# A graph layer on one core: the copy of the transposes goes from ScalarE to VectorE, 56 columns a step in place of 52, columns from step 12 in place of 18

## The chip, the cores and the metric

The kernel runs on one core of one Trainium2 chip. The metric is the device time of one execution in microseconds; lower is better. Engines are named as the profile names them: PE (TensorE), DVE (VectorE), ACT (ScalarE), POOL (GpSimd), SP (SyncE, which only issues transfers here). A row with a "q" behind the engine (ACTq, DVEq, SPq) belongs to that engine's sequencer: what it issues or loads into its registers.

## The reference, cut to what matters

```python
x, src, dst, ef          # 12500 x 64 nodes; 212500 edges, sorted by dst; 212500 x 32 edge features
msg  = relu(concat(x[src], x[dst], ef) @ mW1 + mb1) @ mW2 + mb2     # hidden width 128
agg  = segment_sum(msg, dst, 12500)
upd  = relu(concat(x, agg) @ uW1 + ub1) @ uW2 + ub2
out  = layernorm(x + upd)                                           # over the 64 features
```

Everything is float32. The kernel sums the hidden rows after the relu and multiplies by `mW2` (folded into `uW1`) only once per node.

## The kernel before, in words

The edges are cut into 554 groups of 384 (three tiles of 128 edges). Since the edges are sorted by destination, the edges of one group end in a window of at most 32 nodes. The first matmul of a group has 128 contraction rows: 64 features of the source node, 32 rows of a one-hot of the destination within the window, 32 edge features. Its weights `own_wm` hold the matching rows of `mW1` and, in the middle, 32 rows of the table `by_dst` (the product of every node with the destination part of `mW1`), loaded anew for each group (`window`, L430).

**Steps.** The main loop makes one step per group. Step k does on PE three parts of three groups: `turn(k)` transposes the gathered rows and the one-hots of group k (L466, three transposes into the PSUM tile `own_ps`); `hidden(k-3)` multiplies the operand columns of group k-3 by `own_wm` (L492, into `own_pre`); `sums(k-6)` adds the relu'd rows of group k-6 by the one-hots (L521, into `own_ps` behind the transposes). Behind the step ACT copies the transposes and the sums in one instruction from `own_ps` into `own_operands` (L479, 96 rows or, for a group whose features come as columns, 32 rows, by 513 elements). DVE makes the relu (L503, 128 x 384, `own_pre` to `own_h`) and the one-hots of group k+6 (L440, `own_rows`). SP stores the sums in one of two node tables `by_node` (L455) and loads the window of group k+4.

**Where the features come from.** There are three ways. POOL gathers rows of `x` from HBM with one indirect transfer per tile (L194), `AHEAD` groups ahead of the step, into a ring of `RING` groups. SP fetches two single rows a step for the third tile of 8 groups (L783, `own_side`). And for 71 of the 554 groups ("columned" groups) nothing is gathered: the whole transposed node table lies in SBUF (`own_xc`, each column behind a column of zeros, so that two nodes can be joined by an addition), and DVE and ACT copy the 384 columns one source node at a time. Each step copies 52 columns of the next columned group: DVE 28 as 14 additions of two columns each (L725, parts of 12, 8 and 8), ACT 24 one at a time (L728, parts of 8, 4, 4, 4, 4). The addresses of the columns are known only at run time: ahead of each part its engine loads that many addresses into registers with one TENSOR_LOAD (L702, eight steps' addresses lie in one `index` tile).

**What sets the order.** The order on each engine is written out by hand, in the order of the calls in the loop. `step` waits on PE for the last users of the PSUM slots and for the operands; `follow` issues what comes behind a part. The start differs: until step 15 each step also loads one sixteenth of the node table (`bit`: `src_sb` L256 and `own_xc` L258 on SP, a row of ones L235 on ACT), since a column may come from any node, columns begin only at step `BEGIN` = 18, when all bits are in. Until step 24 each step makes 512 rows of `by_dst` (`projected`: PE L407, ACT copy L410 into one of three buffers `t`, store L411 on SP). `window` waits for every store of `by_dst` issued so far. At step 8 (`CHECKED`) DVE checks once that the edges are sorted. Every 22 or 23 groups 512 nodes are complete, and `update` runs for them in twelve stages, one per step: both tables read back (`found`), joined on PE (L571), a count and a relu on ACT (L588, L621), a copy on DVE (L598), and the norm (L637 to L652). In the last ten steps (`SHORT`) the parts of a step run apart, without columns.

## Time and profile before

| | |
|---|---|
| three timed runs | 1846.92 to 1851.61 us, median 1848.74 us |
| the profiled execution's own time | 1847.94 us |
| its span | 1846.2 us |
| granted PE clock, mean over the span | 0.939 |
| busy share of PE, DVE, ACT, POOL | 76%, 62%, 87%, 74% |
| moved by DMA | 137.63 MB |

How to read it: "busy" counts instructions that the engine executes. Register loads and the issuing of transfers belong to the sequencers and are not counted as busy, so an engine can be held up with a low busy share. Rows of a timeline give start and length in us, then in brackets the idle time ahead of the row and what ended it; neighbouring rows of one kind are merged ("x24"). Rows of one line give its durations as minimum, median and maximum in ns, and then the starts of its first and its last instruction.

### The profile page before, as it was taken

How to read it: one execution, taken by the hardware profiler on the slowest of the kernel's cores; microseconds unless marked ns; L12 is line 12 of the kernel's file. 1: busy time of each engine (PE TensorE's matmuls, PEld its weight loads, DVE VectorE, ACT ScalarE, POOL GpSimd, SP SyncE). 2: the span in 40 equal slices, each digit the busy share in tenths (PEclk: the TensorE clock that was granted, in tenths of full speed). 3: DMA queues.
4: the chain of work that ended last, by engine and by line, in shares of the span. 5: the costliest groups of instructions: out<-in, count | busy, mean ns of one | idle time of the engine just before them, and what ended most of it. 6: DMA issues, size and time to landing. Idle time of an engine off the chain costs nothing. (4 is left out here: it accounts for less than half of the span.)

```text
span 1846.2 us, 57017 instructions
## 1 busy us (share of the span) xinstructions
PE 1402.9 (76%) x9841; PEld 1112.0 (60%) x9841; DVE 1151.3 (62%) x9034; ACT 1602.8 (87%) x13268; POOL 1362.1 (74%) x1447
## 2 busy tenths in 40 slices
PE   3677677877878878768778778777778778788677
PEld 3565565666656656556566566656656556566565
DVE  2315566666666666666666666666666666666652
ACT  2338799999999999899999999989999989989962
POOL 7777577777777777777777777777777777777772
PEclk9759899999999999999999999999989999999999
DMA  6653333333333333333333333333323333333331
GB/s 148 137 132 90 69 74 65 69 76 65 69 75 66 73 72 64 72 61 74 74 65 70 75 64 69 74 64 68 78 63 67 76 63 69 76 63 70 75 65 39
DMA packets 197393, 137.63 MB, mean 75 GB/s; under 512 B 62855, under 2 KB 172653, under 8 KB 196957
## 3 DMA queue, kind: packets, MB, share of 16 engines
q1 hardware_dynamic: 150166, 85.91, 18.7%
q0 software_dynamic: 46080, 47.25, 15.5%
q14 instruction: 288, 2.35, 0.4%
q8 instruction: 85, 1.39, 0.3%
q10 hardware_dynamic: 774, 0.72, 0.2%
HBM read 105.70 MB, written 28.00 MB: 72 GB/s over the span
## 5 line engine op out<-in xcount | busy, mean ns | idle before, releaser
L194 POOL DMA_INDIRECT own_rows<-in_x,src_sb x1440 | 1361.3, 945 | 451.0 <-issue 191.1
L728 ACT ACTIVATE own_operands<-own_xc 64x1 f32 x12576 | 1288.7, 189 | 16.5 <-issue 5.0
L725 DVE TENSOR_TENSOR own_operands<-own_xc 64x2 f32 x7344 | 666.9, 149 | 499.7 <-issue 496.3
L466 PE MATMUL own_ps<-own_ident,own_rows 128*96 128x128 f32 x1653 | 297.8, 292 | 329.9 <-ACT own_operands L728 208.6
L521 PE MATMUL own_ps<-own_h,own_rows 128*32 128x129 f32 x3322 | 491.3, 285 | 4.1 <-ACT own_operands L479 1.9
L492 PE MATMUL own_pre<-own_wm,own_operands 128*128 128x128 f32 x3322 | 490.2, 287 | 0.0
L466 PEld LDWEIGHTS own_ps<-own_ident,own_rows 128*96 128x96 f32 x1653 | 173.0, 133 | 460.4 <-ACT own_operands L728 273.1
L492 PEld LDWEIGHTS own_pre<-own_wm,own_operands 128*128 128x128 f32 x3322 | 443.8, 203 | 2.3 <-issue 1.4
L479 ACT ACTIVATE own_operands<-own_ps 96x513 f32<-96x513 f32 (+2 forms) x554 | 321.1, 580 | 96.0 <-PE own_ps L521 68.5
L503 DVE TENSOR_SCALAR own_h<-own_pre 128x384 f32<-128x384 f32 x553 | 300.4, 543 | 148.2 <-PE own_ps L521 106.9
L521 PEld LDWEIGHTS own_ps<-own_h,own_rows 128*32 128x32 f32 x3322 | 330.5, 113 | 82.7 <-issue 8.6
L440 DVE TENSOR_TENSOR own_rows<-iota,dlc 128x96 f32<-128x96 f32 x554 | 133.7, 242 | 0.1
L571 PE MATMUL u_ps<-own_ident,found 128*1 128x128 f32 (+1 forms) x768 | 100.2, 281 | 19.4 <-DMA found<-by_node 19.0
L571 PEld LDWEIGHTS u_ps<-own_ident,found 128*1 128x1 f32 (+1 forms) x768 | 74.4, 138 | 36.6 <-issue 14.7
L407 PE MATMUL u_ps<-w1b,own_xc 65*128 65x128 f32 x196 | 41.6, 375 | 51.1 <-DMA own_xc<-in_xT_spaced 22.6
L410 ACT ACTIVATE t<-u_ps 128x512 f32<-128x512 f32 (+1 forms) x25 | 14.7, 587 | 70.9 <-DMA by_dst<-t 38.9
L407 PEld LDWEIGHTS u_ps<-w1b,own_xc 65*128 65x128 f32 x196 | 35.4, 268 | 58.3 <-issue 30.5
L576 PE MATMUL u_ps<-own_xc,ux 65*128 65x512 f32 (+1 forms) x50 | 28.5, 650 | 24.1 <-DVE agg L598 24.1
L627 PE MATMUL u_ps<-same,own_xc 65*128 65x64 f32 x192 | 39.6, 288 | 0.5 <-ACT u L621 0.5
L616 PE MATMUL u_ps<-agg,wc 128*128 128x512 f32 (+1 forms) x50 | 39.8, 890 | 0.0
L628 PE MATMUL u_ps<-u,u 128*128 128x64 f32 x192 | 37.1, 275 | 0.0
L627 PEld LDWEIGHTS u_ps<-same,own_xc 65*128 65x128 f32 x192 | 30.3, 197 | 5.7 <-issue 4.2
(92 smaller groups left out, 312.8 us busy)
## 6 DMA issues: line engine op xcount, KB each, us to landing
own_operands<-in_efT SPq DMA_DIRECT2D x138, 192.0 KB
own_rows<-in_x,src_sb POOLq DMA_INDIRECT x1440
by_node<-own_operands SPq DMA_DIRECT2D x554, 32.2 KB
own_side<-in_x SPq DMA_DIRECT2D x1024, 0.2 KB
found<-by_node SPq DMA_DIRECT2D x46, 258.0 KB
own_wm<-by_dst SPq DMA_DIRECT2D x554, 16.0 KB
by_dst<-t SPq DMA_DIRECT2D x24, 256.0 KB
own_xc<-in_xT_spaced SPq DMA_DIRECT2D x12, 358.5 KB
```

Source lines behind the costliest of these rows:

```text
L194: nc.gpsimd.indirect_dma_start(out=s[:p, j, :D], out_offset=None, in_=x[:, :], in_offset=bass.IndirectOffsetOnAxis(ap=src_sb[:p, g * TG + ...
L407: nc.tensor.matmul(ps[:, j], xc[: D + 1, base + j * P :][:, :P], w1b, start=True, stop=True)
L440: places_by[g] = nc.vector.tensor_tensor(own.s[g % RING][:, :, D:], iota.unsqueeze(1).to_broadcast([P, TG, W]), dlc[:, g * TG : (g + 1) * ...
L466: nc.tensor.transpose(xt[:, j * P : j * P + p], sides[g] if g in sides and j == TG - 1 else s[:p, j, :], ident[:p, :p])
L479: after(nc.scalar.activation(t[r, c : c + n], ps[r, AT : AT + n], AF.Copy), step))]
L492: nc.tensor.matmul(pre[:p, j, :], t[:, c + j * P : c + j * P + p], wm[g % NW], start=True, stop=True)
L503: relu_by[g] = [nc.vector.tensor_scalar(h, pre, 0.0, None, ALU.max)]
L521: nc.tensor.matmul(ps[D : D + W, BANK : BANK + ROW], s[:p, j, D:], h[:p, j, :], start=j == 0, stop=j == len(sizes) - 1)
L571: nc.tensor.matmul(ps[:, k * P : (k + 1) * P], t[:, k, w], ident, start=j == 0, stop=j == 1)
L627: nc.tensor.matmul(y[:p, k], xc[: D + 1, nodes[k]], same, start=True, stop=False)
L725: by[engine] = nc.vector.tensor_tensor(o, one, other, ALU.add)
L728: by[engine] = nc.scalar.activation(o, x_at, AF.Copy)
```

## The change

- `tensor_copy` on DVE takes the place of ACT's copy of the transposes (L479 before, L482 and L483 after) for the groups 16 to 543; the first 16 and the last 10 stay on ACT.
- ACT copies 28 columns a step (8, 4, 4, 4, 4, 4), one part of four more; with DVE's 28 that is 56 a step.
- Columns begin at step 12. 77 groups get their features as columns, so POOL has 18 gathers less.
- The sixteen bits of the node table are loaded two per step in the steps 0 to 7; the load of the far part of `dst_cols` goes from ahead of the loop to step 1, and the arithmetic on it (`relative`) to step 8.
- `window(g)` waits only for the stores of `by_dst` of the chunks up to `max(1, g - 6)`, and `t` has four buffers.
- In a step with all three parts the relu of `hidden` is recorded (`later`) behind the first six additions of columns, not behind the step.
- The gathers run 15 groups ahead, not 16 (ring of 19), the small tiles of the check lie in a spare row of `own_xc`, and the first nodes as floats are kept in `first_i`. The nodes 11776 to 12287 are updated as 128 and 384, not 256 and 256.

```diff
-AHEAD = 16
+AHEAD = 15
 RING = AHEAD + 4
...
-BEGIN = 18
+BEGIN = 12
 CHECKED = 8
 VCOLS = (12, 8, 8)
-ACOLS = (8, 4, 4, 4, 4)
+ACOLS = (8, 4, 4, 4, 4, 4)
...
-    for e in [*range(CH, whole, CH), whole - CH // 2, whole, N]:
+    for e in [*range(CH, whole, CH), whole - CH * 3 // 4, whole, N]:
...
-    rowp = ctx.enter_context(tc.tile_pool(name="rows", bufs=3))
+    rowp = ctx.enter_context(tc.tile_pool(name="rows", bufs=4))
...
-        written.append(after(nc.sync.dma_start(
-            by_dst[base : base + n * P, :].rearrange("(n p) h -> p n h", n=n), t[:, :n])))
+        written[c] = after(nc.sync.dma_start(
+            by_dst[base : base + n * P, :].rearrange("(n p) h -> p n h", n=n), t[:, :n]))
...
-        after(wm_by[g], *written, *([hidden_by[g - NW]] if g >= NW else []))
-        written.clear()
+        needed = [written.pop(c) for c in sorted(written) if c <= max(1, g - 6)]
+        after(wm_by[g], *needed, *([hidden_by[g - NW]] if g >= NW else []))
...
-            copies = [ordered_by_steps(
-                after(nc.scalar.activation(t[r, c : c + n], ps[r, AT : AT + n], AF.Copy), step))]
+            out_t, in_ps = t[r, c : c + n], ps[r, AT : AT + n]
+            copies = [ordered_by_steps(after(
+                nc.vector.tensor_copy(out_t, in_ps) if NEAR_GROUPS <= g < G - SHORT
+                else nc.scalar.activation(out_t, in_ps, AF.Copy), step))]
...
-            users[part][(g + ahead_of[part]) % SLOTS] = follow(did[-1])
+            def followed(part=part, g=g, follow=follow):
+                users[part][(g + ahead_of[part]) % SLOTS] = follow(did[-1])
+
+            if part is hidden and len(parts) == 3:
+                later.append(followed)
+            else:
+                followed()
...
-    nc.sync.dma_start(dlc_i[:, near:], a["dst_cols"][:, near:])
     update_weights()
     weights(NW)
     inputs(1)
-    relative(NEAR_GROUPS, G)
...
-        if k < BITS:
-            bit(k)
+        for i in range(2 * k, min(2 * k + 2, BITS)):
+            bit(i)
         if 1 < k < len(TABLE):
             projected(k)
+        if k == 1:
+            nc.sync.dma_start(dlc_i[:, near:], a["dst_cols"][:, near:])
         if k == CHECKED:
+            relative(NEAR_GROUPS, G)
...
         fetch(0)
+        while later:
+            later.pop()()
         window(k + SB)
```

On DVE one step in the middle of the program stands like this before (`own_h` is the relu, `own_operands<-own_xc` the additions of columns, `own_rows` the one-hots):

```order
L503 TENSOR_SCALAR own_h<-own_pre 128x3x128
L702 TENSOR_LOAD index
L725 TENSOR_TENSOR own_operands<-own_xc 64x2 x6
L440 TENSOR_TENSOR own_rows<-iota,dlc 128x3x32
L702 TENSOR_LOAD index
L725 TENSOR_TENSOR own_operands<-own_xc 64x2 x4
L702 TENSOR_LOAD index
L725 TENSOR_TENSOR own_operands<-own_xc 64x2 x4
```

And a step at the same place of the changed program:

```order
L482 COPY own_operands<-own_ps 96x513
L706 TENSOR_LOAD index
L729 TENSOR_TENSOR own_operands<-own_xc 64x2 x6
L507 TENSOR_SCALAR own_h<-own_pre 128x3x128
L442 TENSOR_TENSOR own_rows<-iota,dlc 128x3x32
L706 TENSOR_LOAD index
L729 TENSOR_TENSOR own_operands<-own_xc 64x2 x4
L706 TENSOR_LOAD index
L729 TENSOR_TENSOR own_operands<-own_xc 64x2 x4
```

The copy stands where the relu stood, ahead of the load of 12 addresses, and the relu stands behind the six additions that this load serves.

On ACT a step before is the copy (L479) and five parts of columns, each behind its load of 8 or 4 addresses:

```order
L479 ACTIVATE own_operands<-own_ps 96x513
L702 TENSOR_LOAD index
L728 ACTIVATE own_operands<-own_xc 64x1 x8
L702 TENSOR_LOAD index
L728 ACTIVATE own_operands<-own_xc 64x1 x4
L702 TENSOR_LOAD index
L728 ACTIVATE own_operands<-own_xc 64x1 x4
L702 TENSOR_LOAD index
L728 ACTIVATE own_operands<-own_xc 64x1 x4
L702 TENSOR_LOAD index
L728 ACTIVATE own_operands<-own_xc 64x1 x4
```

In the changed program it is six parts of columns and no copy:

```order
L706 TENSOR_LOAD index
L732 ACTIVATE own_operands<-own_xc 64x1 x8
L706 TENSOR_LOAD index
L732 ACTIVATE own_operands<-own_xc 64x1 x4
L706 TENSOR_LOAD index
L732 ACTIVATE own_operands<-own_xc 64x1 x4
L706 TENSOR_LOAD index
L732 ACTIVATE own_operands<-own_xc 64x1 x4
L706 TENSOR_LOAD index
L732 ACTIVATE own_operands<-own_xc 64x1 x4
L706 TENSOR_LOAD index
L732 ACTIVATE own_operands<-own_xc 64x1 x4
```

One load of four addresses and four columns came, one copy with a wait on PE went.

On SP one early step before (load of a bit, store of `by_dst`, window, store of sums):

```order
L256 DMA src_sb<-in_src 128x101
L258 DMA own_xc<-in_xT_spaced 64x1436
L411 DMA by_dst<-t 128x4x128
L430 DMA own_wm<-by_dst 32x512
L455 DMA by_node_181<-own_operands 64x516
```

And step 7 of the changed program:

```order
L257 DMA src_sb<-in_src 128x101
L259 DMA own_xc<-in_xT_spaced 64x1434
L257 DMA src_sb<-in_src 128x101
L259 DMA own_xc<-in_xT_spaced 64x1436
L413 DMA by_dst<-t 128x4x128
L432 DMA own_wm<-by_dst 32x512
L457 DMA by_node_176<-own_operands 64x516
```

Two bits stand ahead of the store where one stood. On POOL the gathers before and after are these:

```order
L194 DMA own_rows<-in_x,src_sb 128x64 x1439
L194 DMA own_rows<-in_x,src_sb 20x64
```

```order
L195 DMA own_rows<-in_x,src_sb 128x64 x1421
L195 DMA own_rows<-in_x,src_sb 20x64
```

1440 became 1422.

More of the change, by code (lines that the diff above doesn't have):

```diff
@@ L150, in ordered @@
     ident, wm = own.ident, own.wm
+    spare = own.xc[96:97, :]
     xc = own.xc[:, 1 : 2 * NP + 1].rearrange("p (n s) -> p n s", s=2)[:, :, 0]
@@ L276, in ordered @@
     halves = [(0, G // 2), (G // 2, G)]
-    firsts_f = [own.pre[k][:, : g1 - g0] for k, (g0, g1) in enumerate(halves)]
+    all_firsts = first_i.bitcast(F32)
+    firsts_f = [all_firsts[:, g0:g1] for g0, g1 in halves]
     for f, (g0, g1) in zip(firsts_f, halves):
@@ L293, in ordered @@
     relative(0, NEAR_GROUPS)
-    high = temp.tile([1, G], F32, name="high")
+    high = spare[:, 0 * G : 1 * G]
     nc.vector.memset(high, float(N - 1))
@@ L298, in ordered @@
         nc.vector.memset(high[:, g0:g1], float(CH * (1 + max(1, g0 - 6)) - W))
-    start_f = temp.tile([1, G], F32, name="start_f")
+    start_f = spare[:, 1 * G : 2 * G]
     start_b = const.tile([1, G, 2], I32, name="start_b")
@@ L338, in ordered @@
     store_by = {}
-    written = []
+    written = {}
     up = found_p = None
@@ L356, in ordered_edges @@
         nc.vector.tensor_scalar(off, dlc, W - 1.0, 0.0, ALU.is_le, ALU.add, accum_out=valid[:, 1:2])
-        low = temp.tile([1, G], F32, name="low")
+        low = spare[:, 2 * G : 3 * G]
         opens = [0, *(closes for *_, closes in PLAN)]
@@ L363, in ordered_edges @@
         nc.vector.memset(high[:, 0:1], 0.0)
-        wrong = temp.tile([1, 2, G], F32, name="wrong")
+        wrong = spare[:, 3 * G : 5 * G].rearrange("o (k g) -> o k g", k=2)
         nwrong = temp.tile([1, 2], F32, name="nwrong")
         first_f = start_f
-        nc.vector.tensor_copy(first_f, first_i[0:1, :])
+        nc.vector.tensor_copy(first_f, all_firsts[0:1, :])
         nc.vector.tensor_tensor(wrong[:, 0], first_f, low, ALU.is_lt)
@@ L803, in ordered @@
     ahead_of = {turn: 0, hidden: TO_HIDDEN, sums: TO_SUMS}
-    with_sums, unstored = set(), []
+    with_sums, unstored, later = set(), [], []
     def step(*work):
```

## The prediction

> **What bounds the kernel now.** I read the page's first part, then the pace of POOL against the pace of the steps, then the steps themselves, engine by engine.
>
> ```profile
> PE 1402.9 (76%) x9841; PEld 1112.0 (60%) x9841; DVE 1151.3 (62%) x9034; ACT 1602.8 (87%) x13268; POOL 1362.1 (74%) x1447
> ```
>
> No engine is full by its busy time, so the pace has to be looked for elsewhere. Two views of the busy time by stretch, the first for the gathers (L194), the second for the relu (L503, one per step):
>
> ```profile
> 210.00:1000.00 790.00, 597.32 (x633) 0.96 0.33 70
> 1000.00:1780.00 780.00, 589.78 (x625) 0.95 0.33 69
> ```
>
> ```profile
> 0.00:84.40 84.40, 5.00 (x9) 0.88 0.63 143
> 210.00:1000.00 790.00, 137.79 (x254) 0.96 0.33 70
> 1000.00:1780.00 780.00, 135.00 (x249) 0.95 0.33 69
> ```
>
> POOL makes a gather every 790 / 633 = 1.248 us without a break. A step has 1440 / 554 = 2.6 gathers, 3.24 us, and steps take 790 / 254 = 3.11 us: steps are the quicker of the two in the middle, and eat up the lead that the gathers won in the slow start. Both nearly bind; a gain needs both to get shorter. First and last starts of the gathers, and of ACT's columns:
>
> ```profile
> L194 POOL DMA_INDIRECT own_rows<-in_x,src_sb x1440: 898/944/1312, 2.9 to 1813.0; - x180
> L728 ACT ACTIVATE own_operands<-own_xc x12576: 185/188/206, 129.3 to 1783.4; 64x1 f32 x200
> ```
>
> The columns span (1783.4 - 129.3) / (12576 / 24 = 524 steps) = 3.157 us a step; 62.8 us lie behind them to the end of the span. What makes a step, in an undisturbed stretch on ACT:
>
> ```profile
> 1026.14 0.58 ACT L479 ACTIVATE own_operands<-own_ps 96x513 f32<-96x513 f32 x1
> 1026.62 2.44 ACT L728 ACTIVATE own_operands<-own_xc 64x1 f32 x24
> 1028.96 0.58 ACT L479 ACTIVATE own_operands<-own_ps 96x513 f32<-96x513 f32 x1
> 1031.79 0.58 ACT L479 ACTIVATE own_operands<-own_ps 96x513 f32<-96x513 f32 x1
> 1034.61 0.58 ACT L479 ACTIVATE own_operands<-own_ps 96x513 f32<-96x513 f32 x1
> ```
>
> 2.82 us from copy to copy, again and again. The same stretch has two readings. By execution: the copy and 24 columns follow each other without an idle row, so ACT executes all the time. By issue: ACT's sequencer must load 24 addresses and issue 25 instructions, and these are its loads (one of 8 addresses, then ones of 4), with a row of DVE's loads (8 and 12) behind them:
>
> ```profile
> L702 ACTq TENSOR_LOAD <-index x1: 548/548/548, 1022.8 to 1022.8; - x1
> L702 ACTq TENSOR_LOAD <-index x4: 307/308/310, 1020.8 to 1022.3; - x4
> L702 DVEq TENSOR_LOAD <-index x2: 597/722/846, 1018.3 to 1019.2; - x2
> ```
>
> 0.548 + 4 x 0.308 = 1.78 us of loads, which leaves 1.04 us, 41.6 ns for each of 25 issues. Which reading holds is seen where ACT was starved, and where columns come at full speed:
>
> ```profile
> 1702.38 0.60 ACT L479 ACTIVATE own_operands<-own_ps 96x513 f32<-96x513 f32 x1 [2.52 <-PE own_ps L521]
> 1703.01 2.55 ACT L728 ACTIVATE own_operands<-own_xc 64x1 f32 x24
> 1705.46 0.58 ACT L479 ACTIVATE own_operands<-own_ps 96x513 f32<-96x513 f32 x1
> ...
> 1781.23 2.32 ACT L728 ACTIVATE own_operands<-own_xc 64x1 f32 x24
> ```
>
> Full speed is 2.32 us for 24, (2.32 - 0.19) / 23 = 0.093 us from column to column. Behind a copy that came late, with no backlog of issued columns, the same 24 take 2.55 us: the engine waits for its sequencer between the parts. And a load of 4 follows the last after 1.5 / 3 = 0.50 us, while four columns execute in 0.37. I take it that **ACT's sequencer**, with loads and issues, fills the 2.82 us, and that execution only hides it behind the copy's 0.58 us.
>
> DVE is filled in the same way, with its loads in sight as idle time:
>
> ```profile
> 1019.27 0.55 DVE L503 TENSOR_SCALAR own_h<-own_pre 128x384 f32<-128x384 f32 x1
> 1020.10 0.51 DVE L725 TENSOR_TENSOR own_operands<-own_xc 64x2 f32 x6 [0.28 <-issue]
> 1020.53 0.24 DVE L440 TENSOR_TENSOR own_rows<-iota,dlc 128x96 f32<-128x96 f32 x1
> 1021.01 0.36 DVE L725 TENSOR_TENSOR own_operands<-own_xc 64x2 f32 x4 [0.24 <-issue]
> 1021.83 0.38 DVE L725 TENSOR_TENSOR own_operands<-own_xc 64x2 f32 x4 [0.45 <-issue]
> 1022.14 0.54 DVE L503 TENSOR_SCALAR own_h<-own_pre 128x384 f32<-128x384 f32 x1
> ```
>
> 2.87 us from relu to relu, of which 0.97 is idle for issue. The mean of 3.157 lies 0.33 above the quiet step: the stages of the update that come every 22 steps.
>
> **The change part by part.** *POOL:* 18 gathers less at 1.248 us are 22 us, if POOL stays without a break: last start at 2.9 + 1421 x 1.248 = 1776 us, and with the 33 us that lie behind it now an end near 1809. That is a floor, not the sum.
>
> *ACT, per step:* the copy's issue goes (0.04), its wait on PE too; one load of 4 (0.308) and four issues (0.166) come. New quiet step: 0.548 + 5 x 0.308 + 28 x 0.0416 = **3.25 us**, or by the spacing of the loads 2.82 + 0.50 - 0.04 = 3.28. Execution takes 28 x 0.093 = 2.60, so nothing of the loads is hidden behind a long instruction any more, and nothing needs to be: the sequencer alone sets 3.25 to 3.28. I take the upper end, 3.28, since every update adds three ACT instructions. Now ACT has no wait on PE in an ordinary step, so of the 0.33 us for updates most falls away: ACT may lag PE by three steps (a group's columns are wanted by its `hidden`, three steps after its turn) before PE waits, and PE's late stages are caught up in that lag.
>
> *DVE, per step:* it gets the copy of 513 elements. DVE's nearest PSUM copy:
>
> ```profile
> L598 DVE COPY agg<-u_ps 128x512 f32<-128x512 f32 x23 | 15.5, 676 | 0.0
> ```
>
> 0.68 us is the high bound if all of it lay on the path, an issue of about 0.04 the low one. The copy stands ahead of the load of 12 (0.846 us), where the relu's 0.55 is hidden now: the six additions start 0.83 after the relu in the rows above and would start as late behind a copy of 0.68. The relu goes ahead of the one-hots and the load of 8 (0.597): 0.55 + 0.24 against it sticks out by at most 0.2. So DVE's quiet step is 2.87 + 0.04 to 0.24, 2.91 to 3.11, and with its own update work (up to the 0.33 above) 3.2 to 3.4. I take the lower half: below ACT's 3.28 or level with it. If the cover is gone (an update's instruction ahead of the copy), DVE pays up to 0.68 in that step alone.
>
> [...]
>
> *The start.* SP's waits up to 200 us, and a wait of ACT:
>
> ```profile
> SPq L430 <- DMA by_dst<-t: 64.5, 24, 4.2
> ...
> ACT t L410 <- DMA by_dst<-t: 38.9, 11, 6.1
> ```
>
> `window` now asks for old chunks only and `t` has a fourth buffer, so these 64.5 and 38.9 us (the same time, seen by two engines) mostly go. Against that two bits per step queue up in the steps 0 to 7. Columns begin at step 12. The window up to 84.4 us holds nine relus, those of the steps 3 to 11, so step 12 begins here:
>
> ```profile
> 84.41 0.49 PE L466 MATMUL own_ps<-own_ident,own_rows 128*96 128x128 f32 x3
> ```
>
> With the turn, the copy and the loads behind it, the first column comes near 88 us in place of 129.3, if the start is neither quicker nor slower up to there. Low bound 75, if the stores' waits go in steps 2 to 11 too; high bound 110, if the 1.6 MB of four more bits by then, and stores and gathers with them, keep DMA at the 143 GB/s of the row above (a bit is a row of each kind here):
>
> ```profile
> own_xc<-in_xT_spaced SPq DMA_DIRECT2D x12, 358.5 KB
> src_sb<-in_src SPq DMA_DIRECT2D x13, 50.5 KB
> ```
>
> 1.6 MB are 11 us at that rate, and as much again is left for what queues behind them. The check in step 8 gets `relative`, about 3 us of DVE, which is in the 88. Dropping to a ring of 19 costs nothing while steps are slower than gathers.
>
> *The sum.* 77 groups x 384 / 56 = 528 steps of columns, the last step 539; PE needs them at step 543, and before, the last column was that of step 542, so the same 62.8 us follow. 88 + 528 x 3.28 + 62.8 = 1882.6 us of span, 1.7 more for the execution's own time (1847.94 against 1846.2), 0.8 for the median above the profiled run: **1885 us**, 2% slower. The 41 us won at the start are less than the 528 x 3.28 - 524 x 3.157 = 78 us lost along the way. With steps of 3.25 to 3.31 and a first column between 80 and 100 us it is 1861 to 1913.
>
> **The rivals.** *ACT was bound by execution* (faster): then its step falls to 2.60 and DVE's 3.16 (3.12 mean and one issue) or the gathers decide: 88 + 528 x 3.16 + 62.8 + 2.5 = 1822, not below POOL's 1812. For it: the rows of columns show no idle. Against it: the 2.55 behind a late copy. It decides if columns without a copy run at under 3.16 a step.
>
> *DVE binds* (slower still): quiet step 3.11 and updates make 3.37: 88 + 528 x 3.37 + 65 = 1932. For it: the stream on DVE is as tight as ACT's, and it still waits on PE. Against it: the copy lies under a longer load.
>
> *The start is worth more, or the lag absorbs more, than I count* (about level): first column at 75 and 3.23 a step give 75 + 1705 + 65 = 1845. Against it: 3.23 is below the sum of loads and issues.
>
> [...]
>
> **How the numbers follow.** Forecast 0.68, execution-bound 0.13, DVE 0.11, level 0.05, paid in full 0.03. The range 1843 to 1938 takes in the forecast, the level case and DVE's; left out are the fast rival and the far one. This kernel's runs tell about 0.3% from no change, 1843 to 1854: faster 0.15, the same 0.05, slower 0.80.
>
> **What would show it.** ACT: columns with idle rows or gaps between parts, 3.25 to 3.28 us from load of 8 to load of 8, busy share lower although ACT sets the pace. DVE: copies of 0.68 us, six additions 0.83 behind a copy's start, little waiting in front of them or waits on PE. PE waiting for columns of a columned group. First column near 88 us; SP's waits on `by_dst` gone. I am wrong if ACT's steps are under 3.2, or if DVE's sequence from copy to copy is longer than ACT's.

## The result: 7% slower, 92 us beyond the forecast

| | before | after |
|---|---|---|
| median of the timed runs | 1850.17 us (1846.92 to 1855.73) | 1977.08 us (1969.58 to 1984.37) |
| span of the profiled execution | 1846.2 us | 1974.9 us |
| granted PE clock, mean | 0.939 | 0.937 |
| gathers on POOL | 1440 | 1422 |

The ratio is 1.0696, 95% interval 1.0661 to 1.0732. The forecast was 1885 us with a range of 1843 to 1938: the sign was right, the size was not.

The first part of the page after, busy time by engine:

```profile
PE 1406.0 (71%) x9841; PEld 1123.1 (57%) x9841; DVE 1453.9 (74%) x9609; ACT 1685.7 (85%) x14948; POOL 1347.4 (68%) x1429
```

DVE has 300 us more than before, ACT 80, POOL 15 less, and no engine is full. So again the pace decides. These are the relus, one a step (busy time by stretch; the count stands in brackets, and a relu that lies across a boundary counts on both sides), before and then after, up to the relu of step 48 and from there to that of step 543:

```profile
84.00:243.00 159.00, 19.99 (x38) 0.80 0.43 97
243.00:1788.00 1545.00, 268.62 (x496) 0.96 0.33 70
```

```profile
84.00:243.00 159.00, 20.75 (x38) 0.84 0.38 87
243.00:1918.00 1675.00, 269.74 (x496) 0.95 0.30 65
```

Between 84 and 243 us both kernels make the same 38 steps, though the columns of one began at 129.3 us and those of the other at 95.3. From the start of the relu of step 48 to that of step 543 it is 3.121 us a step before and 3.382 after (242.7 to 1787.6 and 243.7 to 1917.8 us, 495 steps). These 0.261 x 495 = 129 us are the whole result. The gathers of the same middle stretch, before and after:

```profile
243.00:1780.00 1537.00, 1162.02 (x1231) 0.96 0.33 70
```

```profile
243.00:1780.00 1537.00, 1092.06 (x1156) 0.95 0.30 65
```

Before, POOL makes a gather every 1537 / 1231 = 1.249 us. The longest interval from start to start in this stretch is 1.42 us, so POOL never stands still. But nothing waits for it: none of TensorE's waits in that profile ends with the landing of a gather, and from step 48 on the last packet of every group's gathers landed at least 1.1 us before the group was transposed (median 21 us). The gathers run ahead of the steps, by 19 groups at step 48 and by 4 at step 540. Who sets the steps is seen from who waits for whom between 300 and 1700 us (us in total, times, longest). VectorE and ScalarE before:

```profile
DVE own_h L503 <- PE own_ps L521: 24.8, 14, 3.3
ACT own_operands L479 <- PE own_ps L521: 40.4, 28, 2.7
```

And after:

```profile
DVE agg L602 <- PE u_ps L575: 61.0, 18, 4.9
DVE own_operands L482 <- PE own_ps L525: 36.8, 35, 2.3
ACT own_operands L732 <- PE own_ps L525: 1.0, 2, 0.5
```

After, **ScalarE sets the pace**: it waits 1.0 us for another engine, VectorE 98. Before, it is VectorE that waits least, 24.8 of 1400 us (ScalarE 59.0), and from relu to relu it needs 2.87 us in a quiet step. That is read from the waits; no run shortens VectorE's step. The gathers of the changed kernel come every 1.33 us, and 69 of the intervals are longer than 1.6 us, since gathers now wait for slots of the ring that slow steps give back late: between 300 and 1700 us up to 3.4 us for VectorE's copies and 2.6 for ScalarE's columns, where before no wait for either engine is longer than 0.3. First and last starts after, for gathers and for ACT's columns:

```profile
L195 POOL DMA_INDIRECT own_rows<-in_x,src_sb x1422: 898/944/1641, 3.0 to 1897.1; - x178
```

```profile
L732 ACT ACTIVATE own_operands<-own_xc x14784: 185/187/205, 95.3 to 1911.3; 64x1 f32 x200
```

What a step looks like on ACT now (timeline; in brackets the idle time ahead of a row):

```profile
1000.58 3.06 ACT L732 ACTIVATE own_operands<-own_xc 64x1 f32 x28 [0.25 <-issue]
1003.55 0.28 ACT L648 ACTIVATE rstd<-mv,eps 128x4 f32<-128x4 f32 x1
1003.92 3.07 ACT L732 ACTIVATE own_operands<-own_xc 64x1 f32 x28
1007.24 1.59 ACT L732 ACTIVATE own_operands<-own_xc 64x1 f32 x16 [0.25 <-issue]
1009.04 1.46 ACT L732 ACTIVATE own_operands<-own_xc 64x1 f32 x12 [0.22 <-issue]
1011.03 3.08 ACT L732 ACTIVATE own_operands<-own_xc 64x1 f32 x28 [0.52 <-issue]
```

28 columns now need 3.06 us from start to end, where 27 x 0.093 + 0.19 = 2.70 would be full speed (a row of e15 below has 2.69), and between two steps ACT waits for its own sequencer. From load of 8 to load of 8, 345 of the 491 steps from step 48 on take less than 3.4 us, 311 of them 3.27 to 3.34; the forecast's quiet step was 3.28. The mean is 3.389. Of the 54 us that 491 steps lie above 3.28, 37 come from 125 steps that take 3.5 to 3.65 (the 0.52 ahead of the last row is the start of one).

On DVE the copies are where the prediction put them, and little waits for them: 78.6 us of idle time ahead of 528 copies.

```profile
L482 DVE COPY own_operands<-own_ps 96x513 f32<-96x513 f32 (+1 forms) x528 | 358.8, 680 | 78.6 <-PE own_ps L525 75.5
```

### The profile page after: what moved, and what is told of

It is laid out like the page before. It is cut to its first block, busy times and chain, and to the rows that moved or that the text cites. A ratio compares the mean times of both kernels' runs of the same rounds, so it can differ in the third digit from the quotient of the medians.

```text
span 1974.9 us, 59418 instructions
## 1 busy us (share of the span) xinstructions
PE 1406.0 (71%) x9841; PEld 1123.1 (57%) x9841; DVE 1453.9 (74%) x9609; ACT 1685.7 (85%) x14948; POOL 1347.4 (68%) x1429
## 5 line engine op out<-in xcount | busy, mean ns | idle before, releaser
L732 ACT ACTIVATE own_operands<-own_xc 64x1 f32 x14784 | 1613.2, 189 | 155.1 <-issue 131.5
L195 POOL DMA_INDIRECT own_rows<-in_x,src_sb x1422 | 1346.6, 947 | 549.8 <-issue 319.6
L525 PE MATMUL own_ps<-own_h,own_rows 128*32 128x129 f32 x3322 | 482.6, 282 | 4.0 <-ACT own_operands L483 1.7
L496 PE MATMUL own_pre<-own_wm,own_operands 128*128 128x128 f32 x3322 | 479.7, 283 | 0.0
L496 PEld LDWEIGHTS own_pre<-own_wm,own_operands 128*128 128x128 f32 x3322 | 432.4, 199 | 1.9 <-issue 1.4
L482 DVE COPY own_operands<-own_ps 96x513 f32<-96x513 f32 (+1 forms) x528 | 358.8, 680 | 78.6 <-PE own_ps L525 75.5
L575 PE MATMUL u_ps<-own_ident,found 128*1 128x128 f32 (+1 forms) x768 | 133.9, 341 | 124.3 <-ACT count L592 105.7
L575 PEld LDWEIGHTS u_ps<-own_ident,found 128*1 128x1 f32 (+1 forms) x768 | 106.2, 196 | 144.9 <-ACT count L592 111.6
L602 DVE COPY agg<-u_ps 128x512 f32<-128x512 f32 (+2 forms) x25 | 16.7, 669 | 75.6 <-PE u_ps L575 75.6
L412 ACT ACTIVATE t<-u_ps 128x512 f32<-128x512 f32 (+1 forms) x25 | 14.7, 588 | 52.5 <-DMA by_dst<-t 27.8
L483 ACT ACTIVATE own_operands<-own_ps 96x384 f32<-96x384 f32 (+2 forms) x26 | 13.5, 518 | 36.6 <-PE own_ps L468 20.7
```

Source lines behind the costliest of these rows:

```text
L195: nc.gpsimd.indirect_dma_start(out=s[:p, j, :D], out_offset=None, in_=x[:, :], in_offset=bass.IndirectOffsetOnAxis(ap=src_sb[:p, g * TG + ...
L482: nc.vector.tensor_copy(out_t, in_ps) if NEAR_GROUPS <= g < G - SHORT
L496: nc.tensor.matmul(pre[:p, j, :], t[:, c + j * P : c + j * P + p], wm[g % NW], start=True, stop=True)
L525: nc.tensor.matmul(ps[D : D + W, BANK : BANK + ROW], s[:p, j, D:], h[:p, j, :], start=j == 0, stop=j == len(sizes) - 1)
L575: nc.tensor.matmul(ps[:, k * P : (k + 1) * P], t[:, k, w], ident, start=j == 0, stop=j == 1)
L732: by[engine] = nc.scalar.activation(o, x_at, AF.Copy)
```

## Experiments

"A step" is the mean from the relu of step 48 to that of step 543, as above. Each kernel was timed beside the kernel before.

| kernel | columns DVE + ACT | ACT's parts | copy on | a step, us | median, us | ratio (95%) |
|---|---|---|---|---|---|---|
| before | 28 + 24 | 8, 4, 4, 4, 4 | ACT | 3.121 | 1850.17 | 1 |
| after | 28 + 28 | 8, 4, 4, 4, 4, 4 | DVE | 3.382 | 1977.08 | 1.070 (1.066 to 1.073) |
| e1 | 28 + 24 | 8, 4, 4, 4, 4 | DVE | 3.122 | 1850.87 | 1.000 (0.999 to 1.002) |
| e4, old start | 28 + 28 | 8, 4, 4, 4, 4, 4 | DVE | 3.398 | 1974.55 | 1.067 (1.062 to 1.072) |
| e3 | 28 + 28 | 8, 4, 4, 4, 4, 4 | ACT | 3.437 | 2017.86 | 1.092 (1.088 to 1.097) |
| e2 | 28 + 28 | 14, 14 | DVE | 5.298 | 2966.68 | 1.605 (1.599 to 1.610) |
| e14 | 28 + 28 | 16, 12 | DVE | 3.108 | 1839.82 | 0.996 (0.994 to 0.997) |
| e15 | 28 + 28 | 16, 12 | ACT | 3.186 | 1879.42 | 1.016 (1.013 to 1.020) |
| e16, before | 28 + 24 | 16, 8 | ACT | 3.125 | 1850.85 | 1.001 (0.999 to 1.003) |
| e13 | 28 + 32 | 16, 16 | DVE | 3.303 | 1933.61 | 1.045 (1.041 to 1.049) |
| e17 | 32 + 28 | 16, 12 | ACT | 3.237 | 1901.72 | 1.030 (1.026 to 1.033) |
| e18 | 32 + 28 | 16, 12 | DVE | 3.278 | 1923.29 | 1.042 (1.040 to 1.044) |

Theory A: ScalarE's sequencer sets the step of the changed kernel, with its register loads and issues. Rivals: its execution (B), VectorE with the copy (C).

### Four columns fewer (e1)

```diff
-ACOLS = (8, 4, 4, 4, 4, 4)
+ACOLS = (8, 4, 4, 4, 4)
```

> The changed kernel with 52 columns a step (8, 4, 4, 4, 4 on ScalarE) in place of 56: one register load of four and four columns a step go from ScalarE, and everything else (copy on VectorE, columns from step 12, eight loading steps) stays. Theory A, ScalarE's sequencer sets the step: 0.308 + 4 x 0.0416 = 0.47 us a step go, 3.439 falls to about 2.97 on ScalarE, and VectorE with its copy (2.91 to 3.11 in a quiet step) or GpSimd (about 1438 gathers x 1.248 = 1795 us and what stands around them) is next: 1830 us (1812 to 1870), below the kernel before. Rival C, VectorE with the copy and its coupling to TensorE sets the step: nothing of it is touched, 1977 us (1950 to 1985).

Measured: 1850.87 us, the time of the kernel before. Relus and then gathers of this run:

```profile
243.00:1788.00 1545.00, 269.53 (x495) 0.98 0.32 70
```

```profile
L195 POOL DMA_INDIRECT own_rows<-in_x,src_sb x1440: 894/944/1641, 2.9 to 1816.5; - x180
```

One load of four and four columns are worth 126 us. Theory C is out: VectorE's work, the copy included, is the same as in the changed kernel, and the 126 us are gone. A's range holds, its 1830 isn't reached. From 300 to 1700 us VectorE waits 5.8 us for TensorE and ScalarE 106.5 us for others, so VectorE, the next in A's list, has the steps. Near the end the gathers hold them back as well; these are TensorE's waits for gathers, all of them behind 1500 us:

```profile
PE own_ps L468 <- DMA own_rows<-in_x,src_sb: 16.0, 11, 2.4
```

With 52 columns the copy on VectorE and the new start together bring nothing: VectorE's steps are no shorter on average (3.122), and the 1440 gathers end at 1816.5, with 34 us behind them as before.

### The old start (e4)

```diff
-BEGIN = 12
+BEGIN = 18
...
-        for i in range(2 * k, min(2 * k + 2, BITS)):
-            bit(i)
+        if k < BITS:
+            bit(k)
...
-        needed = [written.pop(c) for c in sorted(written) if c <= max(1, g - 6)]
+        needed = [written.pop(c) for c in sorted(written)]
```

Three buffers `t` and the old places of `dlc_i` and `relative` as well.

> The changed kernel with the start of the kernel before: columns begin at step 18, the features are loaded in sixteen steps, a window waits for all stores of the table so far, three buffers for the table's rows; 56 columns a step and the copy on VectorE stay. As the prediction had it, the first column comes at 129 and not 95 us, and six steps fewer carry columns (four fewer than 528 by the count of columns): +34 - 4 x 3.44 = +20 us, 1997 us (1990 to 2010). If instead the early steps with columns are slow because they run into the table's stores and the loads (about 4.4 us each between 95 and 200 us), part of it is got back: 1977 (1970 to 1985).

Measured: 1974.55 us beside 1977.08, no difference. The columns and, from step 48 on, the relus of this run:

```profile
L732 ACT ACTIVATE own_operands<-own_xc x14588: 185/187/205, 125.6 to 1912.9; 64x1 f32 x200
```

```profile
243.00:1922.00 1679.00, 269.26 (x495) 0.95 0.30 64
```

The first column comes 30 us later, and no time is lost by it. The relu of step 48 starts at 242.7 us before, at 243.7 after, at 241.9 in e1, at 239.6 with the old start: wherever columns begin, step 48 comes at 240 to 244 us. So the 41 us of the prediction's first term don't exist as a gain. All these runs have one break of 8 to 13 us in their gathers near 192 us, while TensorE waits for the first read-back of the node tables (`found`: 11.1 us before, 10.3 after, 7.4 with the old start). No experiment took out what else paces the steps up to there; what the rows show of it stands in the next part.

### The copy back on ScalarE (e3)

```diff
-                nc.vector.tensor_copy(out_t, in_ps) if NEAR_GROUPS <= g < G - SHORT
-                else nc.scalar.activation(out_t, in_ps, AF.Copy), step))]
+                nc.scalar.activation(out_t, in_ps, AF.Copy), step))]
```

> The changed kernel with the copy of the transposes back on ScalarE in every step; 56 columns and the new start stay. Theory A: ScalarE's sequencer issues one more instruction, 0.03 to 0.04 us a step, and the copy can't be issued before TensorE's step has ended; 528 x 0.04 = 21 us at least, 1998 us (1990 to 2050). Rival C, the copy on VectorE (0.68 us each, 359 us in all) is what lengthened the step: VectorE gets back up to 0.68 us a step, and the time falls below 1977, towards 1930.

Measured: 2017.86 us, 41 us slower than with the copy on VectorE. Rival C had it faster. The move of the copy alone is a gain at 56 columns. A had 21 us at least and 1998 (1990 to 2050): the sign is right, the size low.

How much of the copy's 0.68 us lies on VectorE's path this run can't tell, because ScalarE is the bound in it (24 us of idle time in all ahead of its 14784 columns). VectorE's quiet step does: 2.87 us without the copy (before) and 2.93 with it (e14 below), so 0.06 us are paid.

### The same columns in two register loads (e2)

```diff
-ACOLS = (8, 4, 4, 4, 4, 4)
+ACOLS = (14, 14)
```

> The changed kernel with ScalarE's 28 columns in two parts of 14, not in six (8, 4, 4, 4, 4, 4): the same columns are executed, with two register loads a step in place of six. Theory A, the sequencer sets the step: a load of n registers fits 72 + 59 n ns in the trace, so 2 x 0.90 = 1.80 in place of 0.546 + 5 x 0.308 = 2.09, and the issue of n columns fits 61 + 29 n ns, 2 x 0.47 = 0.94 in place of 1.18: 2.75 a step against 3.28, the step goes to VectorE or GpSimd, about 1835 us (1810 to 1880). Rival B, ScalarE's execution of 28 columns and what they read sets it: not changed, 1977 (1960 to 1985). Rival C, VectorE with the copy sets it: 1977 as well, with ScalarE then idle for 0.5 us a step.

Measured: 2966.68 us, 50% slower than the changed kernel, which no theory had. ACT's timeline, and then the loads at its two places:

```profile
1001.50 1.41 ACT L732 ACTIVATE own_operands<-own_xc 64x1 f32 x14 [0.29 <-issue]
1004.99 1.41 ACT L732 ACTIVATE own_operands<-own_xc 64x1 f32 x14 [2.08 <-issue]
1006.69 1.41 ACT L732 ACTIVATE own_operands<-own_xc 64x1 f32 x14 [0.29 <-issue]
```

```profile
L706 ACTq TENSOR_LOAD <-index x1: 3018/3018/3018, 1001.9 to 1001.9; - x1
```

```profile
L706 ACTq TENSOR_LOAD <-index x1: 1220/1220/1220, 1005.4 to 1005.4; - x1
```

Two loads of 14 registers take 1.22 and 3.02 us, in turn, through the whole run. The loads (1.22 + 3.02) and the issues (2 x 0.47, the estimate of the expectation) make 5.18 us, and steps take 5.2. ACT stands idle for 2.4 us of each. So the step of the sequencer is the step of the kernel, as A says, while execution (B) and VectorE (C) are the same as in the changed kernel. The line through ScalarE's loads of 4 and 8 (0.31 and 0.55 us), from which I had worked out 0.90 for a load of 14, was wrong to be used there.

The two loads differ in where their addresses lie: the 1.22 at byte 112 of a step's addresses, the 3.02 at byte 168. 112 is a multiple of 16, 168 is not, and of the parts used so far each had begun at a multiple of 16 and had a multiple of four addresses. So I took as a rule, an estimate fitted to these two loads and to the 0.31 and 0.55 us of 4 and 8: 0.07 us for the load, and from a multiple of 16 bytes 0.059 us for each register of a full four; a remainder costs 0.217 us each, and so does every register of a load that begins elsewhere (8 bytes off is all that was run), there without the 0.07.

### The rule on trial (e8)

```diff
-ACOLS = (8, 4, 4, 4, 4, 4)
+ACOLS = (6, 6, 8, 8)
```

> The changed kernel with ScalarE's 28 columns in parts of 6, 6, 8 and 8 (byte offsets 112, 136, 160 and 192 in a step's addresses). By the rule of the multiples of 16 bytes: the first 6 take 0.07 + 4 x 0.059 + 2 x 0.217 = 0.74 us, the second, off the multiple, 6 x 0.217 = 1.30, the 8 and 8 0.55 each. If only the count decides (not a multiple of four, slow as a whole), both loads of 6 take the same. ScalarE's step is then 3.14 of loads and 1.07 of issues, about 4.2 us, and the time near 2420 us (2350 to 2500).

In this run and the seven others called e5 to e12, the kernel before itself took 2531 us and not 1850; so of e8 only the durations of its loads are used. The load of 6 at byte 112, then the one at byte 136:

```profile
L706 ACTq TENSOR_LOAD <-index x1: 757/757/757, 1003.5 to 1003.5; - x1
```

```profile
L706 ACTq TENSOR_LOAD <-index x1: 1342/1342/1342, 1004.5 to 1004.5; - x1
```

0.757 and 1.342 us against 0.74 and 1.30 by the rule; the two loads of 8 take 0.543 and 0.547. That only the count decides is out, since both have six registers.

### Eight kernels at 2531 us (e5 to e12)

e5 and e9 are one kernel, later run again as e14; e6 and e10 became e15, e7 and e11 became e16; e12 became e17. Their edits stand with those runs.

> The changed kernel with ScalarE's 28 columns in two parts of 16 and 12 (counts that are multiples of four, byte offsets 112 and 176 in a step's addresses, multiples of 16), not in six. In the run with 14 and 14 the part at byte 112 took 1.22 us and the one at byte 168 3.03. Rule on trial: a register load from an address that is a multiple of 16 bytes goes in fours at 0.059 us a register, what is left over or starts off such an address at 0.217 a register (12 x 0.059 + 0.07 + 2 x 0.217 = 1.21; 14 x 0.217 = 3.04). By it the loads here take 72 + 59 n ns, 1.02 and 0.78, and ScalarE's quiet step is 2.74 in place of 3.28. Theory A, ScalarE's sequencer alone made the changed kernel slow: GpSimd decides again, 1422 gathers x 1.248 + 3 ahead + 16 in gaps + 33 behind = 1827 us (1822 to 1845). Rival C, VectorE with the copy stands right behind at 3.1 to 3.2 a step: 1850 to 1880. If a load of more than 12 is slow whatever its place, over 2500.

> As the run with parts of 16 and 12, and the copy of the transposes back on ScalarE. Theory A: ScalarE's quiet step is 2.74 + 0.04 = 2.78, still under GpSimd's pace (1422 x 1.248 = 1775 us for 554 steps, 3.20 a step): 1827 us (1822 to 1850), as with the copy on VectorE, so that the place of the copy is worth nothing once the loads are short. Rival C: VectorE without the copy has 0.1 to 0.2 us a step more room, and this run is 20 us or more faster than the one with the copy on VectorE.

> The kernel before with ScalarE's 24 columns in two parts of 16 and 8, not in five (8, 4, 4, 4, 4); nothing else. ScalarE's quiet step by its sequencer: 1.02 + 0.55 of loads, 0.53 + 0.30 + 0.04 of issues, 2.44 in place of 2.82. If the kernel before was bound by GpSimd, whose 1440 gathers follow each other at 1.248 us from 2.9 to 1813 us, nothing comes of it: 1848 us (1843 to 1852). If it was bound by ScalarE, as the prediction's first part has it, 0.38 a step or what is left of it up to the next bound goes: 1780 to 1830.

> The changed kernel with ScalarE's 28 columns in two parts of 16 and 12 again, because in its first run the kernel before itself took 2531 us and not 1850. Theory A (ScalarE's sequencer alone made the changed kernel slow, GpSimd's 1422 gathers decide next): 1827 us (1822 to 1845). Rival C (VectorE with the copy stands right behind, 3.1 to 3.2 a step): 1850 to 1880.

> Parts of 16 and 12 with the copy of the transposes on ScalarE, again. Theory A: ScalarE's quiet step is 2.78, GpSimd decides: 1827 us (1822 to 1850), as with the copy on VectorE. Rival C: 20 us or more faster than the one with the copy on VectorE.

> The kernel before with ScalarE's 24 columns in two parts of 16 and 8, again. If the kernel before was bound by GpSimd's 1440 gathers back to back: 1848 us (1843 to 1852). If it was bound by ScalarE: 1780 to 1830.

> 60 columns a step: VectorE 32 in two parts of 16, ScalarE 28 in two of 16 and 12, the copy of the transposes on ScalarE, the start of the changed kernel. 528 x 60 / 384 = 82 groups as columns, about 1407 gathers. GpSimd's floor: 1407 x 1.248 + 52 = 1808 us. ScalarE's quiet step 2.78 and VectorE's (2.18 of loads and 0.85 of issues) 3.03 lie under the 1808 / 554 = 3.26 a step that this leaves. Theory A: 1810 us (1805 to 1835), faster than both kernels. If the waits of the engines on each other in the update steps add up instead, 1850 or more.

Measured: 2462.19, 2471.42 and 2464.67 us for e5 to e7, 2597.44 for e8, 2461.66, 2470.55, 2467.89 and 2472.70 for e9 to e12, each beside 2531 for the kernel before. 52, 56 and 60 columns, the copy here or there: all seven with short loads lie within 11 us. What differs between these seven hardly shows there, and for these questions the runs are inconclusive. What is seen in them: SyncE and ScalarE were held up between single instructions. In e11 ScalarE stands idle for its own sequencer 1.14 and 1.22 us ahead of columns between 1000 and 1012 us, where in e16, the same kernel, no such row is longer than 0.51 between 1000 and 1020. A register move of SyncE (L455, 554 of them) takes 29 ns at the median in the undisturbed profile of the kernel before and in e11, and 38 ns at most in the first, 809 in the second. The cause of that stays open.

### Short register loads (e14, e15, e16)

e14:

```diff
-ACOLS = (8, 4, 4, 4, 4, 4)
+ACOLS = (16, 12)
```

> The changed kernel with ScalarE's 28 columns in parts of 16 and 12, now where the kernel before takes 1850 us. Theory A (ScalarE's register loads alone made the changed kernel slow, GpSimd's 1422 gathers decide next): 1827 us (1822 to 1845), faster than the kernel before. Rival C (VectorE with the copy stands right behind, 3.1 to 3.2 a step): 1850 to 1880.

Measured: 1839.82 us, 137 us faster than the changed kernel by that one line, and 0.4% faster than the kernel before (ratio 0.9957, interval 0.9940 to 0.9974). Loads, gathers and relus of this run:

```profile
L706 ACTq TENSOR_LOAD <-index x1056: 766/1000/1472, 92.7 to 1769.5; - x176
```

```profile
243.00:1780.00 1537.00, 1162.67 (x1228) 0.98 0.32 70
```

```profile
243.00:1781.00 1538.00, 269.80 (x495) 0.98 0.32 70
```

Loads of 16 take 1.01 and one of 12 takes 0.78 us (the three between 1001.5 and 1005.2 us), against 1.02 and 0.78 by the rule. The gathers are back at 1537 / 1228 = 1.252 us, none more than 1.43 apart. The time lies in A's range (1822 to 1845), but not for A's reason. GpSimd does not decide: none of TensorE's waits ends with a gather, and from step 48 on every group's rows landed at least 8 us before they were transposed. It is VectorE, rival C's engine, that doesn't wait between 300 and 1700 us, and ScalarE waits for it:

```profile
DVE own_operands L482 <- PE own_ps L525: 2.4, 5, 1.6
ACT own_operands L732 <- DVE own_operands L482: 50.4, 37, 2.1
```

C had the step at 3.1 to 3.2, and 3.108 is its lower end; its 1850 to 1880 was too high. VectorE in quiet steps of this run:

```profile
1001.55 0.66 DVE L482 COPY own_operands<-own_ps 96x513 f32<-96x513 f32 x1
1002.41 0.55 DVE L729 TENSOR_TENSOR own_operands<-own_xc 64x2 f32 x6 [0.20 <-issue]
1002.88 0.54 DVE L507 TENSOR_SCALAR own_h<-own_pre 128x384 f32<-128x384 f32 x1
...
1004.48 0.68 DVE L482 COPY own_operands<-own_ps 96x513 f32<-96x513 f32 x1
```

2.93 us from copy to copy, and the six additions start 0.86 us behind the copy's start. The copy does lie under the load of 12 addresses.

e15 is e14 with the copy on ScalarE, by the edit of e3.

> Parts of 16 and 12 with the copy of the transposes on ScalarE. Theory A: ScalarE executes 28 columns and the copy, 28 x 0.093 + 0.58 = 3.2 us, at GpSimd's pace of 3.2 a step or just above it: 1827 to 1880, and not faster than with the copy on VectorE. Rival C: 20 us or more faster than with the copy on VectorE.

Measured: 1879.42 us, 40 us slower than e14; the same 41 us as with long loads. Here it is execution, the prediction's rival, that binds ScalarE: 28 columns follow the copy without an idle row, 3.08 us a step, and between 300 and 1700 us ScalarE waits 0.4 us for another engine.

```profile
1008.75 0.60 ACT L482 ACTIVATE own_operands<-own_ps 96x513 f32<-96x513 f32 x1
1009.25 2.69 ACT L731 ACTIVATE own_operands<-own_xc 64x1 f32 x28
1011.84 0.58 ACT L482 ACTIVATE own_operands<-own_ps 96x513 f32<-96x513 f32 x1
```

e16 is the kernel before with two loads on ScalarE:

```diff
-ACOLS = (8, 4, 4, 4, 4)
+ACOLS = (16, 8)
```

> The kernel before with ScalarE's 24 columns in two parts of 16 and 8, nothing else. If the kernel before was bound by GpSimd's 1440 gathers back to back: 1848 us (1843 to 1852). If it was bound by ScalarE: 1780 to 1830.

Measured: 1850.85 us, ratio 1.0009, interval 0.9992 to 1.0027. The quiet step on ScalarE fell, though to 2.70 and not to 2.44, because execution comes next (copy 0.48 and 24 x 0.093):

```profile
1003.45 2.32 ACT L728 ACTIVATE own_operands<-own_xc 64x1 f32 x24
1005.67 0.58 ACT L479 ACTIVATE own_operands<-own_ps 96x513 f32<-96x513 f32 x1
1006.15 2.32 ACT L728 ACTIVATE own_operands<-own_xc 64x1 f32 x24
```

0.12 us in each of 495 steps would have been 59 us, had ScalarE been the bound. None of it shows, so ScalarE, from which the prediction read the step, was not the bound of the kernel before. The gathers explain it for the last part only. TensorE waits for them 24 times, the first at about step 400:

```profile
PE own_ps L466 <- DMA own_rows<-in_x,src_sb: 33.6, 24, 3.7
```

Up to step 350 every group's rows had landed 8 us or more before they were transposed, and still the steps take 3.10 us as against 3.11 before. What is the same there is VectorE: its quiet step from relu to relu is 2.87 us in both, longer than ScalarE's 2.82 and 2.70.

### Sixty columns (e13, e17, e18)

Three ways to take 15 more gathers from POOL. e13, copy on VectorE:

```diff
-VCOLS = (12, 8, 8)
-ACOLS = (8, 4, 4, 4, 4, 4)
+VCOLS = (16, 12)
+ACOLS = (16, 16)
```

> 60 columns a step: VectorE 28 in two parts of 16 and 12, ScalarE 32 in two parts of 16, the copy of the transposes on VectorE, the start of the changed kernel. ScalarE's quiet step by the rule of the multiples of 16 bytes: 2 x 1.02 of loads and 2 x 0.53 of issues, 3.10, with 0.10 for late instructions 3.20; GpSimd's 1407 gathers leave 1808 / 554 = 3.26 a step. Where the kernel before takes 1850 us: 1810 to 1850 by theory A; 1880 or more if VectorE with the copy decides. Where the kernel before takes 2531 us, nothing of this can be read, and the time lies at 2460 to 2480 like that of the other kernels with short loads.

Measured: 1933.61 us, in the range of the rival, but not by VectorE: between 300 and 1700 us VectorE waits 128 us for TensorE, and ScalarE for no other engine. 200 of its columns stand in one row, 0.102 us each:

```profile
999.84 20.32 ACT L732 ACTIVATE own_operands<-own_xc 64x1 f32 x200
```

The row hides a wait. A column takes 0.187 us and the next starts 0.093 behind its start, so a delay of up to 0.09 us leaves no idle time to be seen. At 695 of 846 parts between 300 and 1700 us a column starts 0.18 to 0.22 us behind the one before it. A load of 16 begins when six columns of the part before have started, and the ten that are left, 0.93 us, don't cover its 1.01 (as in e14). From load to load it is 1.60 us, 3.20 a step, and with the pauses of the last section and the update's rows 3.303. So it is the load and the columns in turn, and not the columns alone.

e17, `VCOLS = (16, 16)`, `ACOLS = (16, 12)`, copy on ScalarE:

> 60 columns a step: VectorE 32 in two parts of 16, ScalarE 28 in parts of 16 and 12, the copy of the transposes on ScalarE. In the run with 32 columns on ScalarE and no copy the columns followed each other without idle time, 3.2 us a step; here 28 x 0.093 + 0.58 = 3.2 of execution again, and 3.2 + 0.1 for late instructions is above GpSimd's 1808 / 554 = 3.26 by a hair: 1850 (1810 to 1930). If execution on ScalarE were free, GpSimd's floor of 1808.

Measured: 1901.72 us, in the range, 52 above its middle value. ScalarE has the same work as in e15, and the step is 3.237 in place of 3.186: between 300 and 1700 us VectorE with its 32 columns waits for no other engine, ScalarE 8.1 us. VectorE decides, with ScalarE's execution right behind it. e18, the same with the copy on VectorE:

> 60 columns a step: VectorE 32 in two parts of 16 and the copy of the transposes, ScalarE 28 in parts of 16 and 12 and no copy. With 56 columns and parts of 16 and 12 on ScalarE the gathers ran without a break from 250 us on, and where the steps had lost time to catch up they took 2.8 us. VectorE now gets 4 columns more, 0.14 of loads and 0.05 of issues: 3.0 at most, ScalarE stays at 2.8. Both lie under GpSimd's pace with 1407 gathers (1407 x 1.25 + 3 + 19 + 37 = 1818 us, 3.26 a step). Theory: GpSimd alone decides, 1820 us (1812 to 1835), faster than the kernel before by 1.6%. If VectorE with 32 columns and the copy decides (3.3 a step and more): 1860 to 1930.

Measured: 1923.29 us. The rival is right: with 32 columns and the copy VectorE decides (it waits 1.0 us for others between 300 and 1700 us, ScalarE 134), 3.0 to 3.1 us from copy to copy in quiet steps and 3.28 in the mean; my 3.0 at most was too low, and so was the allowance for the rest.

```profile
1001.02 0.68 DVE L482 COPY own_operands<-own_ps 96x513 f32<-96x513 f32 x1
1001.93 0.65 DVE L729 TENSOR_TENSOR own_operands<-own_xc 64x2 f32 x8 [0.23 <-issue]
...
1003.46 0.65 DVE L729 TENSOR_TENSOR own_operands<-own_xc 64x2 f32 x8 [0.26 <-issue]
1004.04 0.68 DVE L482 COPY own_operands<-own_ps 96x513 f32<-96x513 f32 x1
```

e14 with its 56 columns is the best of all: its quiet steps are 2.80 us on ScalarE and 2.93 on VectorE, its gathers land at least 8 us ahead of the transposes, and it is 0.4% below the kernel before.

## Why the prediction was wrong, step by step

**What bounds the kernel before: half right.** The prediction saw that steps and gathers "both nearly bind", and that holds: no wait for a gather before, and as soon as ScalarE's loads are shorter (e16) gathers are waited for near the end. It took ScalarE's sequencer for what makes the step. That was wrong: e16 shortens it and the step stays, and VectorE's quiet step, 2.87 us in the prediction's own rows, is the longer one. The 0.33 us between quiet step and mean were put down to the update, and no gather is in them. That most of it would fall away for ScalarE was right: it waits 1.0 us for others between 300 and 1700 us in place of 59.0.

**ScalarE's quiet step: right.** 3.28 forecast, 3.27 to 3.34 in 311 of 491 steps. e2 and e14 show that its sequencer sets it: the same 28 columns make a step of 5.2 us with slow loads, and with short ones the step passes to VectorE.

**The start: this step failed.** The first column came at 95.3 us (88 forecast, 75 to 110 as bounds), but "the 41 us won at the start" are no gain: the 36 steps from there to step 48 take 4.13 us each and not 3.28, as these rows of the changed kernel show (1007 columns are 36 steps, 13778 are 492), and e4 without the new start is as fast.

```profile
95.00:243.70 148.70, 109.76 (x1007) 0.83 0.36 83
243.70:1911.30 1667.60, 1503.23 (x13778) 0.95 0.30 65
```

36 x 0.85 = 31 us and 7 for the later first column make 38 of the 92 us. 18 of the 31 lie in the steps 12 to 23, which take 4.77 us each. There ScalarE also copies rows of `by_dst`, 12 x 0.58 = 7 us, and waits 11.1 us for their stores, and the prediction priced these steps like the later ones. 9 lie in the one step of 11.96 us in which TensorE waits for the first read-back.

**One price for every step: mis-sized.** 492 steps at 1667.6 / 492 = 3.389 in place of 3.28 are the other 54 us. "Every update adds three ACT instructions" was to be covered by the upper end of 3.25 to 3.28; 17 us went there and elsewhere, 37 into 125 steps of 3.5 to 3.65, a stall that the trace of before had too and that I hadn't counted (last section).

**VectorE and the copy: right.** The quiet step was put at 2.91 to 3.11 (2.93 in e14), the additions 0.83 behind the copy (0.86), and it doesn't bind the changed kernel, where VectorE waits 98 us for TensorE. In e1 and e14, with a shorter step on ScalarE, VectorE binds. The copy on ScalarE costs 41 and 40 us more. The case of a copy paid in full, which got a chance of 0.03, no run shows: the whole 0.68 us on top of the 3.121 a step of before would be 3.80, the step is 3.382, and 0.06 us of the copy are paid in e14's quiet step.

**SyncE's waits on `by_dst`: wrong.** They were to go with the new condition in `window`. They stay at 60.1 us (64.5 before); the ScalarE wait fell from 38.9 to 27.8.

```profile
SPq L432 <- DMA by_dst<-t: 60.1, 24, 5.5
```

```profile
ACT t L412 <- DMA by_dst<-t: 27.8, 13, 7.4
```

**The rivals.** Execution on ScalarE didn't bind the kernel before and doesn't bind the changed one; it binds in e15. VectorE doesn't bind the changed kernel; it does in e1, e14, e17 and e18. The tail of 62.8 us was 63.6.

## What to carry to other kernels

If one producer's rows follow each other at one interval from the first to the last (1.249 us for the gathers before), it never waits, but that doesn't say that anyone waits for it: look for the waits that its landings end, and how far it runs ahead. Of two engines whose quiet steps are nearly equal (2.82 and 2.87 here), the longer sets the step, and making the other quicker brought nothing (e16: ratio 1.0009). A merged row without idle time can hide waits that are shorter than one instruction (up to 0.09 us ahead of a column in e13). A start that is made quicker is worth what it leaves at the first point where both versions must wait for the same thing, not the time by which its first row comes earlier. And a line through two sizes of one operation holds for the forms it was drawn from: 14 registers, off the multiple of 16 bytes, took 3.02 us where the line gave 0.90.

## What the hardware showed that I had not expected

- **Where a register load begins counts.** On ScalarE a load of 16, 12 (e14), 8 or 4 registers (before) from a multiple of 16 bytes takes 1.01, 0.78, 0.55 and 0.31 us; 14 registers take 1.22 from such a place and 3.02 from one 8 bytes off it (e2), 6 registers 0.76 and 1.34 (e8). Six loads for 28 registers take 2.09 us, two of 16 and 12 take 1.79; with their issues that is what tells 1977 us from 1840.
- **A stall every 130 or so records.** From one load's start to the next ScalarE's sequencer takes 0.27 to 0.30 us longer (median 0.28) mostly behind every 122 to 133 of its records, which was every 12.6 us in the changed kernel. In e2, where steps take 5.2 us, it comes behind 120 to 137 records, every 21 to 25 us. So in these two runs it goes with the number of instructions and not with time. The trace has transfers of 8 KB on a queue that the profile lists as `instruction` (q14): 116 of 129 such pauses of the changed kernel are followed by one of them 0.8 to 2.2 us later, while a moment taken at random is in 22% of cases. No run here shows what causes the pause. In the changed kernel, where ScalarE's sequencer sets the pace, it lengthens about every fourth step (125 of 491) by some 0.3 us.
- **Single instructions held up.** In the runs at 2531 us single moves of SyncE took up to 0.81 us (e11) and 0.92 (e9) in place of 0.03, and four different kernels with short loads (e5, e6, e7, e12) came out at 2462 to 2473 us, within 0.5% of each other.
